# First pair of graphs: four PSUM buffers, both graphs side by side, adjacency loaded into idle buffers, weights loaded later

## The chip, the cores and the metric

The kernel runs on one core of a Trainium2 chip. The metric is the device time of one execution in microseconds (us). Before the change it is 3160.63 us, the median of three runs (3157.54 to 3173.24). PE is the matrix engine (PEld its weight loads), DVE the vector engine, ACT the scalar engine, POOL the general one; SP only issues DMAs here. L with a number is a line of the kernel before; lines of the changed kernel are named as such.

## What is computed

Sixteen graphs of 1024 nodes with 64 features each pass two layers; each adds its result to its input. Cut to what matters:

```python
# layer 0: thin out the neighbours, then take quantiles over those that stay
neigh = (adj > 0) & ~eye;  rank = cumsum(neigh) - neigh;  nb = neigh.sum(-1)
skip = where(nb > 10, (nb + 1) // 2, 1)
rem = neigh & (skip > 1) & (rank % skip == skip - 1) & mask;  rem = rem | rem.T
nd = where(rem, 0, adj with ones on its diagonal) > 0
s = sort(where(nd, h, inf))                   # h = relu(layernorm(x)); per node and feature
agg = 0.25 * quantile(s, 0.25) + 0.5 * quantile(s, 0.5) + 0.25 * quantile(s, 0.75)
x = x + (relu((h + agg) @ W1 + b1) @ W2 + b2) * mask
# layer 1: three graph convolutions  relu(adj @ (x @ W) + b), each with batch norm, then Wl
```

## The kernel before, in words

**Pairs and stages.** The graphs are handled in eight pairs. For each pair there is a preparation (`prepare`, L585) and then seven blocks of nodes, ordered by degree, each gathered and sorted. `prepare` loads x, does the layernorm (`room`, L560 to L568), stores h, and calls `prepare_one` (L654) for each graph of the pair, one after the other. That has these steps, and yields between them:

1. Eight row blocks of the adjacency (`a`, 128x1024 f32, 512 KB, two buffers; L664, issued by SP). ACT takes the sign into `edge` (L671), DVE checks that all values are 0 or 1 (`junk_v` and `odd`, L673), PE turns the block over in eight 128x128 products (`ptE`, L678), ACT evicts it into `edgeT` (L681).
2. `edgeT` is stored to memory for layer 1 (`adjT_d`, L684); then DVE clears its diagonal (L686), which overwrites what the store reads and so waits for it. `chunk_sums` (PE `tot` L646, ACT `sums` L651), then the degrees (`nbp` L691, and small DVE operations L695 to L707 that give `back` and `look`).
3. For each of eight row blocks: PE forms running counts (`cs`, L716 and L721), ACT evicts them as `stays` (L725), DVE compares (L726).
4. For each row block: PE adds up the parts (`q`, L736 to L747), ACT evicts the live edges into `edge` with a count (`nv`, L752).
5. The nodes are ranked by their number of neighbours: `key` (L758), PE spreads it (`keys`, L763), eight ACT passes count who lies above (L770), and `place` (L773) is the rank.
6. POOL scatters the rows of `edge` to memory by `place` (`live_d`, L778), eight DMAs.
7. `find_live` (L788): POOL fetches the rows back in their new order (`lp`, two buffers, L794), PE turns them over (`pt` L809), ACT evicts them into `liveT` (L812), then sums, `nvs` (L822) and a check of bounds (`by` L829, evicted at L833).
8. `number_slots` (L838): PE numbers the live neighbours of each node (`pr`, L845 and L847), ACT evicts them into `r0` (the first 592 nodes) or `r1` (L851). `r0` is done in `prepare`, `r1` in `st.number`, which is worked off during the first sort of the pair.

`prepare` ends with the quantile positions `z` (L615 to L618) and `hp`, h split into three bf16 parts (L623 to L628). Then a gather makes one-hot matrices on DVE (`s`, L987) and multiplies them on PE (`pg`, L1018); sort networks on DVE (L935) follow.

**What sets the order.** Each engine works through its instructions in one fixed order, which a scheduler at compile time makes from the order in which the code is written and from its own estimate of the durations. For the first pair the written order is `prepare`, then the first gather, with nothing beside them. From then on `weave` (L1106) steps the preparation of the next pair and the gather of the next block between the sort's instructions, by shares. After the last pair's gather begins, `later` does the dense layers in the same way; it is the only reader of the weights.

**PSUM.** In `prepare` all of `ptE`, `tot`, `nbp`, `cs`, `q`, `keys`, `pt`, `pr` and the like share one tag, `big`, with two buffers of two banks each, in the pool `ps_early`. The rest of PSUM belongs to the pool `ps` of the gather.

**Weights.** Before anything else is written, ACT's queue issues 46 small DMAs with all weights and biases (`weight`, `column`, `row`, `both`, L496 to L518), and DVE and ACT fold the batch norm into a scale and a shift (`bn_s`, L531 to L537). ACT's first passes over the graphs stand behind these in its order.

**Buffers.** The pools `work` (tags `s`, `agg` and others) and `rows` (tags `g`, `t`) belong to gather and sort, and hold nothing while the first pair is prepared.

Of the kernel before, what the change touches and what calls it, by code (L numbers as in the profile page):

```python
# [10 lines left out]
F32 = mybir.dt.float32  # L11
F16 = mybir.dt.float16
BF16 = mybir.dt.bfloat16
F8 = mybir.dt.float8e4
I32 = mybir.dt.int32
U8 = mybir.dt.uint8
AF = mybir.ActivationFunctionType
ALU = mybir.AluOpType
# [4 lines left out]
P = 128  # L23
# [6 lines left out]

SHARES = (10, 9, 17, 24, 20, 13, 0)
STEPS = 7

MAGIC = 8388608.0

# [344 lines left out]
class Steps:  # L380


    def __init__(self, gen):
        self.gen, self.result = gen, None
# [13 lines left out]
            pass  # L398


@with_exitstack
def graph_layers_kernel(ctx: ExitStack, tc: tile.TileContext, ins, out: bass.AP):
    nc = tc.nc
# [89 lines left out]

    odd = const.tile([P, NB, NT], F32, name="odd")

    def weight(name, rows, cols, twice=False):  # L496
        t = const.tile([rows * (1 + twice), cols], F32, name=f"w_{name}")
        for k in range(1 + twice):
            nc.scalar.dma_start(out=t[k * rows : (k + 1) * rows, :], in_=ins[name])
        return t  # L500

    def column(name, rows, twice=False):
        t = const.tile([rows * (1 + twice), 1], F32, name=f"c_{name}")
        for k in range(1 + twice):
            nc.scalar.dma_start(out=t[k * rows : (k + 1) * rows, :], in_=ins[name].rearrange("(p o) -> p o", o=1))
        return t

    def row(name, cols):
        t = const.tile([P, cols], F32, name=f"r_{name}")
        nc.scalar.dma_start(out=t, in_=ins[name].partition_broadcast(P))  # L510
        return t

    def both(t, src):

        nc.vector.memset(t, 0.0)
        for k in range(2):
            half = slice(k * C, (k + 1) * C)
            nc.scalar.dma_start(out=t[half, half], in_=src)  # L518


    w1 = weight("L0_gnn_W1", C, HID, True)
    w2 = weight("L0_gnn_W2", HID, C)
    b1 = column("L0_gnn_b1", HID)
    b2 = row("L0_gnn_b2", C)
    layers = []
    for i in (1, 2, 3):
        wl = const.tile([P, P], F32, name=f"wl{i}")
        both(wl, ins[f"L1_gnn_W{i}"])
        bl, g, be, m, v = (column(f"L1_gnn_{k}{i}", C, True) for k in ("b", "g", "be", "m", "v"))
        s = const.tile([P, 1], F32, name=f"bn_s{i}")  # L530
        nc.vector.tensor_scalar(s, v, BN_EPS, None, ALU.add)  # L531
        nc.scalar.activation(s, s, AF.Sqrt)
        nc.vector.reciprocal(s, s)
        nc.vector.tensor_tensor(s, s, g, ALU.mult)

        nc.vector.tensor_tensor(m, m, s, ALU.mult)
        nc.vector.tensor_tensor(be, be, m, ALU.subtract)  # L537
        layers.append((wl, bl, s, be))
    wlast = const.tile([P, 3, P], F32, name="wlast")
    for i in range(3):  # L540
        both(wlast[:, i, :], ins["L1_gnn_Wl"][i * C : (i + 1) * C, :])
    blast = row("L1_gnn_bl", C)

    biases = {}

# [8 lines left out]
    def rows_of(ap):  # L554
        return ap.rearrange("(t p) c -> p t c", p=P)
# [26 lines left out]
        pass  # L582


    def prepare(p, pools):  # L585


        work, keep, ps = pools
        st = Pair()
        st.p = p  # L590
        room = work.tile([P, 4, 2, NT, C], F32, tag="stays", name="room")
        xt, h, sq = room[:, 0], room[:, 1], room[:, 2].rearrange("p x t c -> p (x t) c")
        for x in range(2):
            nc.sync.dma_start(out=xt[:, x], in_=rows_of(x_d[2 * p + x]))
        flat = "p x t c -> p (x t) c"
        layernorm_relu(work, h.rearrange(flat), xt.rearrange(flat), sq, T2)
        for x in range(2):
            nc.sync.dma_start(out=rows_of(h_d[2 * p + x][:, :]), in_=h[:, x])
        yield
        st.g = {}  # L600
        st.nvs = keep.tile([P, N], BF16, tag="nvs", bufs=2, name="nvs")
        r0 = keep.tile([P, 2, NT, SPLIT], BF16, tag="r0", name="r0")
        r1 = keep.tile([P, 2, NT, N - SPLIT], BF16, tag="r1", name="r1")
        st.r = (r0, r1)
        find_live, number_slots = [], []
        for x in range(2):
            find_live.append((yield from prepare_one(st, x, pools)))
        for x in range(2):
            number_slots.append((yield from find_live[x]()))
            yield from number_slots[x](0)  # L610


        st.z = keep.tile([P, len(TAUS), N], BF16, tag="z", name="z")
        half = work.tile([P, N], F32, tag="a", bufs=2, name="half")
        nc.vector.tensor_scalar(half, st.nvs, 0.498, MAGIC, ALU.mult, ALU.add)  # L615
        nc.vector.tensor_scalar(half, half, MAGIC, None, ALU.subtract)
        for q, (tau, _) in enumerate(TAUS):
            nc.vector.scalar_tensor_tensor(st.z[:, q, :], st.nvs, -tau, half, ALU.mult, ALU.add)  # L618
        yield

        h = work.tile([P, 2, NT, C], F32, tag="a", bufs=2, name="h_again")
        for x in range(2):
            nc.sync.dma_start(out=h[:, x], in_=rows_of(h_d[2 * p + x][:, :]))  # L623
        st.hp = keep.tile([P, 3, 2, NT, C], BF16, tag="hp", bufs=2, name="hp")
        nc.scalar.copy(st.hp[:, 0], h)
        nc.vector.tensor_tensor(h, h, st.hp[:, 0], ALU.subtract)
        nc.scalar.copy(st.hp[:, 1], h)
        nc.vector.tensor_tensor(st.hp[:, 2], h, st.hp[:, 1], ALU.subtract)  # L628
        yield
        st.number = itertools.chain(*(number_slots[x](1) for x in range(2)))  # L630
        return st

    def diagonal(e):

# [19 lines left out]
    def prepare_one(st, x, pools):  # L654
# [5 lines left out]
        edge = work.tile([P, NT, N], F8, tag="byte", bufs=4, name="edge")  # L660
        edgeT = work.tile([P, NT, N], F8, tag="byte", bufs=4, name="edgeT")
        def load(t):
            a = work.tile([P, N], F32, tag="a", bufs=2, name="a")
            nc.sync.dma_start(out=a, in_=adj_d[b, t * P : (t + 1) * P, :])  # L664
            return a
# [3 lines left out]
        for t in range(NT):  # L669
            a, coming = coming, load(t + 1) if t + 1 < NT else None  # L670
            nc.scalar.activation(edge[:, t, :], a, AF.Sign, saturate=False)  # L671
            junk = work.tile([P, N], F8, tag="junk_v", name="junk_v")
            nc.vector.scalar_tensor_tensor(  # L673
                junk, a, 1.0, a, ALU.is_equal, ALU.not_equal, accum_out=odd[:, b, t : t + 1], saturate=False
            )
            pt = ps.tile([P, NT, P], F32, tag="big", bufs=2, name="ptE")
            for u in range(NT):
                nc.tensor.matmul(  # L678
                    out=pt[:, u, :], lhsT=edge[:, t, u * P : (u + 1) * P], rhs=ident_h, start=True, stop=True
                )  # L680
            nc.scalar.activation(edgeT[:, :, t * P : (t + 1) * P], pt, AF.Copy, saturate=False)  # L681
            yield

        nc.sync.dma_start(out=adjT_d[b][:, :, :], in_=edgeT)  # L684
        own = diagonal(edgeT)
        nc.vector.tensor_tensor(own, own, other_h[:, None, :].to_broadcast([P, NT, P]), ALU.mult, saturate=False)  # L686
        yield
# [43 lines left out]
        for t in range(NT):  # L731
            q = ps.tile([P, N], F32, tag="big", bufs=2, name="q")
            for hf in range(NH):
# [15 lines left out]
                        start=False, stop=(u % 4 == 3),  # L749
                    )  # L750

            nc.scalar.activation(  # L752
                edge[:, t, :], q, AF.Relu, bias=bias(-2.0), accum_out=nv[:, t : t + 1], saturate=False
            )
            yield

        key = work.tile([P, NT], F32, tag="key", name="key")
# [30 lines left out]
        def find_live():  # L788
# [16 lines left out]
            for t in range(NT):  # L805
                lp, coming = coming, fetch(t + 1) if t + 1 < NT else None
                pt = ps.tile([P, NT, P], F32, tag="big", bufs=2, name="pt")
                for u in range(NT):
                    nc.tensor.matmul(  # L809
                        out=pt[:, u, :], lhsT=lp[:, u * P : (u + 1) * P], rhs=ident_h, start=True, stop=True  # L810
                    )
                nc.scalar.activation(liveT[:, :, t * P : (t + 1) * P], pt, AF.Copy, saturate=False)  # L812
                yield

            half = slice(x * C, (x + 1) * C)
# [22 lines left out]
            def number_slots(side):  # L838

                j0, j1 = ((0, SPLIT), (SPLIT, N))[side]  # L840
                for u in range(NT):
                    pr = ps.tile([P, N], F32, tag="big", bufs=2, name="pr")
                    for a in range(j0, j1, HALF):
                        sl, o = slice(a, min(a + HALF, j1)), slice(a - j0, min(a + HALF, j1) - j0)
                        nc.tensor.matmul(out=pr[:, o], lhsT=upto, rhs=liveT[:, u, sl], start=True, stop=(u == 0))  # L845
                        if u:
# [1 line left out]
                                out=pr[:, o], lhsT=before[:, u : u + 1].to_broadcast([P, P]), rhs=sums[:, sl],  # L848
                                start=False, stop=True,
                            )  # L850
                    nc.scalar.copy(st.r[side][:, x, u, :], pr[:, : j1 - j0])  # L851
                    if u % 2:
                        yield

# [420 lines left out]
    def general(stack):  # L1275
# [37 lines left out]
        with tc.For_i(0, NB) as b:  # L1313
# [102 lines left out]
            ahead.rest()  # L1416
            Steps(next_layer((one, ps), [out[b]], [adjT], xt, ahead.result)).rest()


    with ExitStack() as stack:  # L1420
        keep = stack.enter_context(tc.tile_pool(name="keep", bufs=1))
        pools = (
            stack.enter_context(tc.tile_pool(name="work", bufs=1)),
            stack.enter_context(tc.tile_pool(name="ps", bufs=1, space=PSUM)),
            stack.enter_context(tc.tile_pool(name="rows", bufs=1)),
        )
        last = len(BLOCKS)
        with ExitStack() as inner:
            early = (
                inner.enter_context(tc.tile_pool(name="early", bufs=1)), keep,  # L1430
                inner.enter_context(tc.tile_pool(name="ps_early", bufs=1, space=PSUM)),
            )
            ahead = Steps(prepare(0, early))
            ahead.rest()
            st = ahead.result
            first, *_ = gather_block(st, 0, pools)
            first.rest()
            for p in range(NP - 1):
# [7 lines left out]
                for n in range(last):  # L1446
# [16 lines left out]
                    else:  # L1463
                        weave(sort_block(st, n, pools), gather_block(st, n + 1, pools), steps)
                st = to_come
            for _ in st.number:
                pass

# [69 lines left out]
```

## Time and profile before

The profiled execution took 3163.56 us; its span, from the first to the last instruction, is 3161.8 us.

| what | value |
|---|---|
| median of the runs | 3160.63 us |
| profiled execution / span | 3163.56 / 3161.8 us |
| PE busy | 2599.2 us (82%), 27849 matmuls |
| DVE busy | 2559.8 us (81%) |
| ACT busy | 1696.2 us (54%) |
| POOL busy | 619.5 us (20%) |
| moved | 177.45 MB |
| mean granted PE clock | 0.915 |

The table of slices of a profile divides the span into 40 equal parts and gives the busy share of each engine in tenths. A row of the timeline reads: start, duration, engine, line, operation, out<-in with their sizes, count, and in brackets the idle time before it and what ended that (`<-DMA a<-in_adj`: a load of the tile `a`). Several like instructions in a row are merged, with their whole stretch as the duration. A row of the windows gives a stretch, its length, and for each engine its busy time in it with the number of instructions.

### The profile page before, as it was taken

How to read it: one execution, taken by the hardware profiler on the slowest of the kernel's cores; microseconds unless marked ns; L12 is line 12 of the kernel's file. 1: busy time of each engine (PE TensorE's matmuls, PEld its weight loads, DVE VectorE, ACT ScalarE, POOL GpSimd, SP SyncE). 2: the span in 40 equal slices, each digit the busy share in tenths (PEclk: the TensorE clock that was granted, in tenths of full speed). 3: DMA queues.
4: the chain of work that ended last, by engine and by line, in shares of the span. 5: the costliest groups of instructions: out<-in, count | busy, mean ns of one | idle time of the engine just before them, and what ended most of it. 6: DMA issues, size and time to landing. Idle time of an engine off the chain costs nothing.

```text
span 3161.8 us, 67201 instructions
## 1 busy us (share of the span) xinstructions
PE 2599.2 (82%) x27849; PEld 1697.4 (54%) x27849; DVE 2559.8 (81%) x5895; ACT 1696.2 (54%) x3292; POOL 619.5 (20%) x545
## 2 busy tenths in 40 slices
PE   2678978898888889885798889888986688977778
PEld 1445655565556556653565566456643456644445
DVE  4149889998999799989998999899976979963332
ACT  4764666567557755774367557745853223332221
POOL 5110161022102200330022103300422530311110
PEclk9779999999899999997899999999987799988989
DMA  4131022111211212122111211211113011122211
GB/s 138 46 104 60 3 67 70 56 55 52 66 57 54 64 56 68 46 72 47 42 64 51 66 56 57 67 56 63 48 36 75 9 41 26 49 55 54 54 54 42
DMA packets 221082, 177.45 MB, mean 56 GB/s; under 512 B 189024, under 2 KB 189152, under 8 KB 216672
## 3 DMA queue, kind: packets, MB, share of 16 engines
q1 hardware_dynamic: 141824, 125.88, 13.1%
q0 software_dynamic: 17408, 37.81, 3.9%
q10 hardware_dynamic: 61536, 9.39, 1.7%
q8 instruction: 219, 3.59, 0.5%
q14 instruction: 95, 0.78, 0.1%
HBM read 124.44 MB, written 48.55 MB: 55 GB/s over the span
## 4 chain that ended last, share of the span: by engine, by line
DVE 40%; PE 29%; ACT 12%; DMA 8%; issue 6%; another core or an unknown queue 2%; POOL 2%; ACTq 1%; DVEq 0%; POOLq 0%; SPq 0%
PE pg L1018 11%; DVE t L935 10%; DVE s L987 9%; DVE g L935 8%; PE pg L1200 5%; ACT junk L770 3%; DMA a<-in_adj 3%; DMA lp<-live_d 3%; DVE junk_v L673 2%; PE pr L845 2%; DVE g_tails L935 1%; DVE t_tails L935 1%; PE keys L763 1%; PE pf L1216 1%
## 5 line engine op out<-in xcount | busy, mean ns | idle before, releaser
L1018 PE MATMUL pg<-s,hp 128*64 128x400 bf16 (+11 forms) x16848 | 1366.5, 313 | 172.3 <-DVE s L987 138.1
L1018 PEld LDWEIGHTS <-hp 128*64 128x64 bf16 x16848 | 894.5, 112 | 553.9 <-issue 109.6
L987 DVE TENSOR_SCALAR s<-r 128x3200 bf16<-128x3200 bf16 (+25 forms) x1312 | 623.6, 521 | 103.6 <-PE pg L1018 74.9
L778 POOL DMA_INDIRECT live_d<-edge,place x128 | 261.1, 2040 | 1354.3 <-DVE place L773 1149.9
L1023 ACT COPY g<-pg 128x400 f32<-128x400 f32 (+10 forms) x384 | 169.0, 443 | 399.4 <-PE pg L1018 363.1
L935 DVE TENSOR_TENSOR t<-g 128x600 f32<-128x600 f32 (+9 forms) x524 | 315.5, 626 | 34.0 <-ACT g L1023 33.2
L1200 PE MATMUL pg<-adjT,xw 128*64 128x512 fp8e4 x2304 | 284.5, 398 | 52.8 <-ACT xw L1185 25.7
L935 DVE TENSOR_TENSOR g<-t 128x96 f32<-128x96 f32 (+16 forms) x555 | 283.2, 537 | 1.2
L1243 POOL DMA_INDIRECT agg<-agg_d,place x128 | 171.2, 1338 | 495.2 <-PE pt L1131 258.2
L671 ACT ACTIVATE edge<-a 128x1024 fp8e4<-128x1024 f32 x128 | 135.1, 1058 | 214.4 <-DMA a<-in_adj 213.9
L1200 PEld LDWEIGHTS <-xw 128*64 128x64 bf16 x2304 | 140.1, 114 | 182.4 <-issue 42.0
L868 ACT ACTIVATE coef<-z,bias 128x200 f32<-128x200 bf16 (+6 forms) x480 | 173.9, 405 | 102.3 <-DVE agg L950 66.0
L935 DVE TENSOR_TENSOR t<-t 128x192 f32<-128x192 f32 (+20 forms) x447 | 207.8, 475 | 0.2
L871 ACT ACTIVATE coef<-coef,wcol 128x200 f32<-128x200 f32 (+7 forms) x512 | 189.6, 403 | 9.3 <-issue 7.1
L673 DVE SCALAR_TENSOR_TENSOR junk_v<-a 128x1024 fp8e4<-128x1024 f32 x128 | 155.4, 1214 | 24.4 <-DMA a<-in_adj 24.4
L845 PE MATMUL pr<-liveT,upto 128*128 128x512 fp8e4 (+2 forms) x384 | 127.4, 350 | 53.1 <-ACT r L851 46.9
L770 ACT ACTIVATE junk<-keys,minus 128x1024 fp8e4<-128x1024 f32 x128 | 144.3, 1128 | 38.1 <-PE keys L763 34.3
L851 ACT CAST r<-pr 128x592 bf16<-128x592 f32 (+1 forms) x256 | 142.5, 585 | 41.1 <-PE pr L847 32.1
L794 POOL DMA_DIRECT2D lp<-live_d x128 | 89.4, 699 | 376.9 <-PE pt L809 319.3
L812 ACT ACTIVATE liveT<-pt 128x1024 fp8e4<-128x1024 f32 x128 | 130.3, 1034 | 50.5 <-PE pt L809 47.1
L752 ACT ACTIVATE edge<-q,bias 128x1024 fp8e4<-128x1024 f32 x128 | 141.8, 1108 | 22.6 <-PE q L747 22.6
L725 ACT ACTIVATE stays<-cs,back 128x1024 f16<-128x1024 f32 x128 | 136.7, 1111 | 31.1 <-PE cs L721 15.9
(182 smaller groups left out, 3879.4 us busy)
## 6 DMA issues: line engine op xcount, KB each, us to landing
a<-in_adj SPq DMA_DIRECT2D x128, 512.0 KB
adjT_d<-edgeT SPq DMA_DIRECT2D x16, 1024.0 KB
lp<-live_d POOLq DMA_DIRECT2D x128, 128.0 KB
adjT<-adjT_d SPq DMA_DIRECT2D x16, 1024.0 KB
room<-in_x SPq DMA_DIRECT2D x16, 256.0 KB
h_d<-room SPq DMA_DIRECT2D x16, 256.0 KB
h_again<-h_d SPq DMA_DIRECT2D x16, 256.0 KB
xt<-in_x SPq DMA_DIRECT2D x16, 256.0 KB
```

Source lines behind the costliest of these rows:

```text
L673: nc.vector.scalar_tensor_tensor(junk, a, 1.0, a, ALU.is_equal, ALU.not_equal, accum_out=odd[:, b, t : t + 1], saturate=False)
L770: nc.scalar.activation(junk, keys, AF.Sign, bias=minus[:, t : t + 1], accum_out=above[:, t : t + 1], saturate=False)
L778: sent = nc.gpsimd.indirect_dma_start(out=live_d[b][:, :], out_offset=bass.IndirectOffsetOnAxis(ap=place[:, b, t : t + 1], axis=0), in_=ed ...
L845: nc.tensor.matmul(out=pr[:, o], lhsT=upto, rhs=liveT[:, u, sl], start=True, stop=(u == 0))
L868: nc.scalar.activation(coef[:, i, :], z[:, at], AF.Abs, bias=bias(rank - (slots + 1) // 2 + tau), scale=sign)
L871: nc.scalar.activation(coef[:, i, :], coef[:, i, :], AF.Relu, bias=wcol[:, q : q + 1], scale=-w)
L935: nc.vector.tensor_tensor(view(bufs, o, n1, n2), view(bufs, a, n1, n2), view(bufs, b, n1, n2), ALU.max if op else ALU.min)
L987: nc.vector.tensor_scalar(s[:, k, :, us, w0:], r[:, :, us, at + w0 : at + W], float(LIVE + 1 + k0 + k), None, ALU.is_equal)
L1018: summed = nc.tensor.matmul(out=pg[x * C : (x + 1) * C, ks, w0:], lhsT=st.hp[:, part, x, u, :], rhs=s[:, ks, x, u, w0:], start=(whole and ...
L1023: nc.scalar.copy(g[:, k0 : k0 + n, :], pg)
L1200: nc.tensor.matmul(out=pg[cs, :], lhsT=part[:, u, cs], rhs=adjT[x][:, u, sl], start=(u == 0 and k == 0), stop=(u == NT - 1 and k == len(xw ...
L1243: nc.gpsimd.indirect_dma_start(out=agg[:, t, x, :], out_offset=None, in_=agg_d[b][:, :], in_offset=bass.IndirectOffsetOnAxis(ap=place[:, b ...
```

## The change

It touches the first pair's preparation, the loading of weights, and which pool exists when:

- **PSUM**: the first pair's preparation gets a pool of its own, `ps_first`, in which the tag `big` has four buffers (all eight banks). It is closed before the pools `ps` and `ps_early` are opened. `r1` of the first pair uses `ps_early` with two buffers.
- **Loads**: for the first pair the sixteen row blocks of the adjacency go into sixteen `homes`, buffers of the gather, the sort and `a` that are idle then, all issued right behind x and h instead of two at a time. The compiled SP order is: x (2), eight loads, the two stores of h, eight loads.
- **Side by side**: the steps of the two graphs alternate, graph 1 beginning when graph 0 has turned over its eight row blocks and stored them.
- **Evictions**: for the first pair every second eviction of `edgeT`, of `q`, of `liveT`, of `r0` and of `r1` is on DVE. The store of `edgeT` is issued by ACT, as 32-bit words.
- **Checks**: the sixteen checks of the first pair are written last; in the compiled DVE order they still stand in the first stage, all ahead of graph 0's `look`.
- **Weights**: they are issued by SP behind the first gather of pair 2 (`behind`), in the loop after pair 1's sorts. In the compiled SP order they stand between the fifth and the sixth load of pair 3's row blocks. The batch norm's operations are in the sort of pair 2. The weights' memsets stay early.

```diff
+WEIGHTS = 1
+def side_by_side(one, other):
+    while one.step():
+        other.step()
...
+    behind = None
+    def load_weight(t, src):
+        tc.add_manual_dep(
+            nc.sync.dma_start(out=t, in_=src).ins, behind.ins.name,
...
     def weight(name, rows, cols, twice=False):
...
-            nc.scalar.dma_start(out=t[k * rows : (k + 1) * rows, :], in_=ins[name])
+            load_weight(t[k * rows : (k + 1) * rows, :], ins[name])
...
-    def prepare(p, pools):
+    def prepare(p, pools, homes=()):
...
+        for k, home in enumerate(homes):
+            nc.sync.dma_start(out=home, in_=adj_d[2 * p + k // NT, k % NT * P : (k % NT + 1) * P, :])
...
+        if homes:
+            one, other = (Steps(prepare_one(st, x, pools)) for x in range(2))
+            for _ in range(4 + NT):
+                one.step()
+            side_by_side(one, other)
+            find_live = Steps(one.result())
+            side_by_side(find_live, other)
+            other.rest()
+            number_slots.append(find_live.result)
+            find_live = Steps(other.result())
+            side_by_side(Steps(number_slots[0](0)), find_live)
+            find_live.rest()
+            number_slots.append(find_live.result)
+            yield from number_slots[1](0)
+            for k, home in enumerate(homes):
+                check(2 * p + k // NT, k % NT, home)
...
+    def evict(st, t, o, i):
+        if st.homes and t % 2:
+            nc.vector.tensor_scalar(o, i, 1.0, None, ALU.mult, saturate=o.dtype != F8)
+        else:
+            nc.scalar.activation(o, i, AF.Copy, saturate=o.dtype != F8)
...
-            nc.scalar.activation(edgeT[:, :, t * P : (t + 1) * P], pt, AF.Copy, saturate=False)
+            evict(st, t, edgeT[:, :, t * P : (t + 1) * P], pt)
...
-        nc.sync.dma_start(out=adjT_d[b][:, :, :], in_=edgeT)
+        if st.homes:
+            nc.scalar.dma_start(out=adjT_d[b][:, :, :].bitcast(I32), in_=edgeT.bitcast(I32))
+        else:
+            nc.sync.dma_start(out=adjT_d[b][:, :, :], in_=edgeT)
...
+            if st.homes and t % 2:
+                nc.vector.tensor_scalar(
+                    edge[:, t, :], q, 3.0, 0.0, ALU.is_equal, ALU.add, accum_out=nv[:, t : t + 1], saturate=False
+                )
...
-                nc.scalar.activation(liveT[:, :, t * P : (t + 1) * P], pt, AF.Copy, saturate=False)
+                evict(st, t, liveT[:, :, t * P : (t + 1) * P], pt)
...
-                    nc.scalar.copy(st.r[side][:, x, u, :], pr[:, : j1 - j0])
+                    evict(st, u, st.r[side][:, x, u, :], pr[:, : j1 - j0])
...
+            homes = []
+            for pool, tag, bufs, free in (
+                (rows, "g", 2, 2), (rows, "g", 2, 2), (rows, "t", 1, 3), (work, "s", 2, 3), (work, "s", 2, 3),
+                (work, "agg", 1, 1), (room, "a", 2, 1), (room, "a", 2, 1),
+            ):
+                home = pool.tile([P, free, N], F32, tag=tag, bufs=bufs, name="home")
+                homes += [home[:, k] for k in range(free)]
+            with tc.tile_pool(name="ps_first", bufs=1, space=PSUM) as ps_first:
+                ahead = Steps(prepare(0, (room, keep, Deep(ps_first, 4)), homes))
+                ahead.rest()
             st = ahead.result
+            pools = work, stack.enter_context(tc.tile_pool(name="ps", bufs=1, space=PSUM)), rows
+            early = room, keep, inner.enter_context(tc.tile_pool(name="ps_early", bufs=1, space=PSUM))
+            st.ps = early[2]
...
                 st = to_come
+                if p != WEIGHTS:
+                    continue
+                behind = st.gathered
...
+                w1 = weight("L0_gnn_W1", C, HID, True)
...
```

## The prediction

> **What bounds the kernel now.** I read the table of 40 slices first (79 us each). DVE is at 9 in most slices; in the first three it is at 4, 1 and 4: there something else sets the pace.
>
> ```profile
> PE   2678978898888889885798889888986688977778
> DVE  4149889998999799989998999899976979963332
> ACT  4764666567557755774367557745853223332221
> PEclk9779999999899999997899999999987799988989
> ```
>
> So only the time until the first gather (some 206 us) is at stake, and from there a lead gained is passed on, because PE and DVE are busy for 189 and 192 us of the 220 between 280 and 500 and follow each other. The windows by stage show what fills the prologue:
>
> ```profile
> 32.00:67.00 35.00, 12.23 (x99) 8.29 (x100) 17.88 (x31) 22.60 (x24) 11.52 (x60) 1.00 0.69 223
> 67.00:91.00 24.00, 19.70 (x186) 13.25 (x184) 7.65 (x18) 20.75 (x28) 0.00 (x0) 1.00 0.15 50
> 91.00:109.00 18.00, 9.12 (x80) 7.88 (x81) 0.18 (x2) 15.77 (x23) 0.00 (x0) 0.67 0.00 1
> 109.00:143.00 34.00, 23.84 (x221) 15.52 (x220) 6.40 (x17) 20.21 (x27) 8.94 (x10) 0.77 0.20 70
> 143.00:161.00 18.00, 8.90 (x80) 7.86 (x80) 2.96 (x5) 15.59 (x23) 3.22 (x6) 0.65 0.28 74
> 161.00:191.00 30.00, 19.08 (x123) 9.82 (x124) 2.87 (x4) 17.97 (x25) 12.75 (x16) 0.61 0.37 106
> ```
>
> Columns: stretch, length, busy us of PE, weight load, DVE, ACT, POOL, then granted clock, DMA share, GB/s. No engine is full; the stages run one after another. The timeline gives the marks that I count from:
>
> ```profile
> 31.57 1.06 ACT L563 ACTIVATE room<-room 128x1024 f32<-128x1024 f32 x1 [1.74 <-DMA wlast<-in_L_gnn_Wl]
> ```
> ```profile
> 67.08 1.10 ACT L725 ACTIVATE stays<-cs,back 128x1024 f16<-128x1024 f32 x1
> ...
> 93.22 1.11 ACT L770 ACTIVATE junk<-keys,minus 128x1024 fp8e4<-128x1024 f32 x1 [2.40 <-PE keys L763]
> ```
> ```profile
> 161.33 0.17 DVE L773 TENSOR_SCALAR place<-above 128x8 int32<-128x8 f32 x1 [12.62 <-ACT junk L770]
> ...
> 195.56 0.69 DVE L615 TENSOR_SCALAR half<-nvs 128x1024 f32<-128x1024 bf16 x1 [29.14 <-ACT nvs L822]
> ...
> 205.80 1.89 DVE L987 TENSOR_SCALAR s<-r 128x3200 bf16<-128x3200 bf16 x2
> ```
>
> ACT does no work on the graphs until 31.57: it issues weights, 46 DMAs at 0.607 us each, 28 us. First `stays` at 67.08, first ranking pass at 93.22, `place` of the two graphs at 109.09 and 161.33, first one-hot `s` at 205.80.
>
> **Edge stage.** The weights leave ACT's head, so ACT starts with the first row block, which landed 4.4 us after its issue. Now DVE is the limit, because the compiled order has all sixteen `odd` checks ahead of graph 0's `look`: 16 x 1.15 (their pitch in the trace) = 18.4; layernorm 1.22+0.2+1.22+1.22+0.25+1.23 = 5.3; constants 2.1; four evictions; the diagonal product 1.25; memsets and small operations 2.5. A DVE eviction from PSUM is not in the trace: its 1024-element f32 rows lie between 0.69 (`half`) and 1.22 (`junk_v`). I take 1.2, since ACT's 1.02 for the same tile lies nearer to it; 4.8 (at 0.69: 2.8). Sum 34.3, from 4.8. The product must wait for the store of `adjT` (4.5 alone; up to 8 beside the loads): some 2 us more. So first `stays` at 41 instead of 67.1: **lead 26**. Loads: 8.4 MB ran at 223 GB/s with two in flight (38 us), single short slices of the trace reach 396 (21 us); the check of the last block comes at 40, so only the slow end costs, up to 5. A second table load (1.28) lies on ACT, which has room.
>
> [...]
>
> **Side by side.** Each later stage is a chain in one engine's order, and the order now mixes two graphs.
> - `stays` and q: 8 x 1.06 + 1.0 on ACT, then what the trace has from last `stays` to `key` (78.7 to 90.84, 12.2) plus six `ptE` groups of graph 1 on PE at 0.6: 3.6. Graph 0's `key` at 41 + 9.5 + 15.8 = 66.3, lead 24.5. Half the q evictions on DVE bring nothing: PE needs 1.4 per block, ACT 1.2 to 1.3.
> - `keys`. PE's order has graph 1's `tot` and `nbp` ahead of graph 0's `keys`. Graph 1's `edgeT` is stored only about 1.5 before `key`; then store 4.6, product 1.25, `tot` 1.9, `sums` 1.05, `nbp` 0.4, `keys` 2.06: first ranking pass at 76.1. **Lead 17**: 7 us go to a new wait. The passes alternate with graph 1's `stays` as they did with its `edgeT`: 15.9, `place` at 92.
> - First `pt`. Scatter and fetch take 12.4 + 2.4 = 14.8 in the trace: 106.8. PE has this `pt` ahead of graph 1's last two `cs`, so it stands still for about 10 us where the old order ran graph 1 under graph 0's scatter. Then `pt` 1.0, two `cs` of 1.7 each (their pace at 119 to 123, with the clock of 0.67 in the stage before), `stays`, `not_equal`, a DVE eviction: 6.8; eight q at 1.4, six `pt` at 0.6, `tot` 1.5, last eviction 1.3: 17.6. Graph 1's `key` at 131.2 against 143.10: **lead 12**.
> - Ranking of graph 1: no longer alternating with eight `liveT` (18.2), but with two `r`, a square and a root: 2.4 + 8.8 + 1.1 + 1.4, and some 1.5 until the first `pr`: 15.2. `place` at 146.4, lead 15.
> - Scatter, fetch, `liveT` of graph 1: fetch-bound (two `lp` buffers, `pt` waits up to 3.3 us on DMA), so split evictions and more PSUM bring nothing: 29.4 as before, 0.5 for graph 0's `pr` between. To the first `s`: 15.05 as before, plus 1, as DVE now has four `r` evictions and all of `z` ahead of `s`. **First `s` at 192, lead 13.5.** Bounds: 4 (slow loads and stores) and 26 (no later loss).
>
> **What is given back behind it.** Eight of the first pair's sixteen `r1` evictions (128x432) go from ACT to DVE, seven of them beside its sort, where DVE is busy 47.4 of 50 us: 7 x 0.5 (0.49 is 432/1024 of 1.15) = 3.5, bounds 0 and 7, as PE holds two `pr` buffers and may wait behind DVE's order. The weights' fifteen small DVE operations now stand in the sort of pair 2: 15 x 0.16 = 2.4, bounds 2 and 5 (three roots on ACT between them). The weights themselves go to SP's queue, which they hold for 28 us between the fifth and the sixth row block of pair 3, with its `mk` and `adjT` store behind them. In the trace the gather that they wait for ends at 838 and the fifth block is issued near 841; the first `v` would land at 841 + 17 x 0.607 + 2 = 853, and DVE comes to its use at 853.6, to the second (861 against 860.6) and the third (868 against 868) about in time. The next check stands some 30 DVE rows later than before. I take 0, bounds 0 and 28.
>
> Sum: 13.5 - 3.5 - 2.4 = 7.6 us. From the profiled execution (3163.6; span 3161.8 and 1.8 around it) 3156; the median of the runs is 2.9 lower: **3153**.
>
> **Rivals.**
> 1. The lead of 26 survives: the two waits in PE's order prove shorter than priced, because the store and the scatter land sooner. For it: PE, DVE and ACT all have room in the prologue; against it: 14.8 and 4.5 us are measured with DMA nearly idle. 26 - 6 = 20: 3141.
> 2. Slower: SP's queue. If its 46 weight issues come later than DVE's rows for them (from a lag of about 1 us, as the three marks show), DVE stands for the rest, at worst all 28 us: 13.5 - 6 - 28 = -20.5: 3181. For it: all three marks are within 1 us, and `a` loads and DVE are in the same fixed order. Against it: each further `v` is due 7 us after the last, as fast as they are issued.
> 3. The change does nothing that lasts: the first gather starts early, but pair 1's preparation does not (in the first 1000 us SP waits 194.8 us until `edgeT` can be stored), and the lead is lost at the first change of pairs: 3160 to 3166.
>
> **Chances.** Forecast 0.50, rival 1 0.27, rival 2 0.11, rival 3 0.12. The measurement tells some 0.5% (15.8 us) from no change: faster is rival 1 and 0.05 of the forecast's own spread, 0.32; slower is rival 2, 0.11; the rest, 0.57. The range takes in rival 1 and rival 3 and the bounds of the lead, and leaves out rival 2: 3134 to 3172; the forecast's own is 3145 to 3160.
>
> **What would show it.** First `edge` on ACT near 6 us instead of 32; first `stays` at 41; `keys` waiting for `nbp`, first ranking pass at 76; PE idle about 10 us ahead of the first `pt` near 107; first `s` at 192; seven `r1` evictions on DVE within the first sort; no DVE wait on `c_L_gnn_v` over 2 us. A first `s` ahead of 185 makes rival 1, a wait of DVE or ACT on weights or on `a` of over 15 us rival 2.

## The result and the profile after

The changed kernel takes 3166.87 us (median of 20 runs, 3144.34 to 3182.04), the kernel before on the same chip 3167.34 us (20 runs, 3156.96 to 3176.8): ratio **0.9996**, 95% interval 0.9978 to 1.0014. No difference can be told. A second set on another chip gave 0.9974 (0.9950 to 0.9997). The median of before differs between the chips used here (3167, 3134, 3139 and 3134 us), so below only ratios to it, times on one chip and times inside one profile are compared.

The profiled execution took 3148.95 us, its span is 3147.2 us. It is the second shortest of the 20; of its 14.6 us less than before's span a part is luck. The 40 slices of its page, 79 us each:

```profile
PE   5379888888898788984987889888986689977778
DVE  6279889998999799999997999799986979963332
PEclk9789899999999899987998999899986899988889
```

DVE's first three digits are 6, 2, 7 instead of 4, 1, 4: the prologue did shrink. The windows of its stages (busy us of PE, weight load, DVE, ACT, POOL, then clock, DMA share, GB/s):

```profile
7.00:42.40 35.40, 15.83 (x128) 10.62 (x129) 29.77 (x65) 22.90 (x25) 22.90 (x57) 1.00 0.71 256
...
75.40:91.00 15.60, 5.59 (x61) 3.82 (x58) 3.10 (x7) 15.01 (x22) 0.02 (x1) 0.81 0.00 1
91.00:106.40 15.40, 1.04 (x9) 0.99 (x10) 0.00 (x0) 0.00 (x0) 8.92 (x10) 0.50 0.25 85
...
141.00:157.00 16.00, 1.39 (x10) 1.12 (x11) 0.17 (x1) 1.42 (x3) 8.95 (x11) 0.50 0.52 148
```

The edge stage is now full of DVE (29.8 of 35.4 us). But there are two stretches of some 15 us, 91 to 106 and 141 to 157, in which little but POOL's scatters and fetches runs; the other engines stand nearly idle. The marks, from ACT's and then DVE's timeline:

```profile
6.88 1.06 ACT L706 ACTIVATE edge<-home 128x1024 fp8e4<-128x1024 f32 x1 [4.84 <-DMA home<-in_adj]
...
42.39 6.13 ACT L762 ACTIVATE stays<-cs,back 128x1024 f16<-128x1024 f32 x6 [4.04 <-DVE bias L544]
...
75.44 1.11 ACT L812 ACTIVATE junk<-keys,minus 128x1024 fp8e4<-128x1024 f32 x1 [3.74 <-PE keys L805]
...
106.44 1.02 ACT L664 ACTIVATE liveT<-pt 128x1024 fp8e4<-128x1024 f32 x1 [15.95 <-PE pt L851]
```
```profile
141.01 0.17 DVE L815 TENSOR_SCALAR place<-above 128x8 int32<-128x8 f32 x1 [0.82 <-ACT junk L812]
...
182.81 1.89 DVE L1029 TENSOR_SCALAR s<-r 128x3200 bf16<-128x3200 bf16 x2
```

The first `s` stands at 182.81 instead of 205.80: **23 us earlier** (187.44 in a second profile of it: 18). So the question is where some 20 us went. To follow them I number ACT's copies `g<-pg`, whose order is the same in every kernel here, and compare the time between two of them. About half of all stretches of four copies agree within 1 us in the four profiles, and a single profile can be off by up to 10 us. Behind the first eight copies, both changed profiles differ from both of before by more than 4 us in two places only, those of the last two rows:

| stretch (copies) | before, two profiles | changed, two profiles |
|---|---|---|
| start to first copy | 213.6, 213.1 | 192.4, 196.4 |
| start to 48 (pair 1's sort) | 520.7, 523.0 | 500.5, 500.8 |
| 103 to 107 | 17.7, 18.5 | 25.0, 26.1 |
| 132 to 140 | 82.4, 71.9 | 86.4, 89.8 |

With the pairs counted from 0, some 20 to 22 us are passed on into pair 1 and most of it is lost beside the sort of pair 2, where pair 3 is prepared and the weights now load. SP's timeline there, in the changed kernel (first and last of the weights; the code and the traces have 48 of these loads, where the description of before and the prediction say 46; the 28 us for them change by about 1):

```profile
784.73 27.34 SPq L699 DMA_DIRECT2D a<-in_adj  x5
812.12 1.83 SPq L509 DMA_DIRECT2D w_L_gnn_W<-in_L_gnn_W  x3
...
843.91 0.59 SPq L509 DMA_DIRECT2D r_L_gnn_bl<-in_L_gnn_bl  x1
844.93 1.19 SPq L699 DMA_DIRECT2D a<-in_adj  x2
```

And ACT's waits in the same stretch (bracket: idle before, and what ended it):

```profile
815.56 1.06 ACT L706 ACTIVATE edge<-a 128x1024 fp8e4<-128x1024 f32 x1 [0.83 <-DMA a<-in_adj]
...
825.93 0.20 ACT L1538 ACTIVATE bn_s<-bn_s 128x1 f32<-128x1 f32 x1 [0.20 <-DVE bn_s L1537]
...
834.33 0.20 ACT L1538 ACTIVATE bn_s<-bn_s 128x1 f32<-128x1 f32 x1 [5.54 <-DVE bn_s L1537]
...
842.01 0.20 ACT L1538 ACTIVATE bn_s<-bn_s 128x1 f32<-128x1 f32 x1 [6.69 <-DVE bn_s L1537]
...
848.80 1.06 ACT L706 ACTIVATE edge<-a 128x1024 fp8e4<-128x1024 f32 x1 [5.87 <-DMA a<-in_adj]
```

Theories: **C**, the clock gives the lead back (mean granted clock 0.911 over the changed kernel's 20 runs, 0.915 in before's first profile); **W**, the weights' new place costs it; **R**, the `r1` evictions on DVE and the new order beside the first sort cost it.

### The profile page after: what moved, and what is told of

Read it like the earlier page. It is cut to its first block, busy times and chain, and to the rows that moved or that the text cites. A ratio compares the mean times of both kernels' runs of the same rounds, so it can differ in the third digit from the quotient of the medians.

```text
span 3147.2 us, 67155 instructions
## 1 busy us (share of the span) xinstructions
PE 2590.4 (82%) x27826; PEld 1705.3 (54%) x27849; DVE 2596.7 (83%) x5943; ACT 1663.0 (53%) x3245; POOL 614.6 (20%) x545
## 4 chain that ended last, share of the span: by engine, by line
DVE 44%; PE 25%; issue 9%; ACT 9%; DMA 6%; POOL 4%; another core or an unknown queue 2%; SPq 1%; DVEq 0%; POOLq 0%; ACTq 0%
DVE t L977 11%; DVE s L1029 10%; DVE g L977 9%; PE pg L1060 9%; PE pg L1242 5%; DVE junk_v L593 3%; DMA lp<-live_d 3%; ACT junk L812 2%; POOL live_d L820 1%; DVE g_tails L977 1%; DMA a<-in_adj 1%; DVE t_tails L977 1%; PE pt L851 1%; POOL agg L1285 1%
## 5 line engine op out<-in xcount | busy, mean ns | idle before, releaser
L820 POOL DMA_INDIRECT live_d<-edge,place x128 | 246.0, 1922 | 1341.1 <-DVE place L815 1130.8
L1285 POOL DMA_INDIRECT agg<-agg_d,place x128 | 178.3, 1393 | 488.9 <-PE pt L1173 310.7
L706 ACT ACTIVATE edge<-a 128x1024 fp8e4<-128x1024 f32 x112 | 118.3, 1058 | 193.5 <-DMA a<-in_adj 193.3
L664 ACT ACTIVATE liveT<-pt 128x1024 fp8e4<-128x1024 f32 x120 | 122.4, 1034 | 84.3 <-PE pt L851 82.5
L851 PE MATMUL pt<-ident_h,lp 128*128 128x128 bf16 x1024 | 81.8, 228 | 93.1 <-DMA lp<-live_d 83.9
L664 ACT ACTIVATE r<-pr 128x592 bf16<-128x592 f32 (+1 forms) x240 | 136.1, 593 | 38.4 <-PE pr L889 29.3
L1247 DVE TENSOR_SCALAR xT<-xT,bn_s,c_L_gnn_be 128x512 f32<-128x512 f32 x48 | 26.1, 544 | 155.0 <-ACT xT L1246 154.9
```

The lines of the kernel that those rows point to most:

```text
L664: nc.scalar.activation(o, i, AF.Copy, saturate=o.dtype != F8)
L820: sent = nc.gpsimd.indirect_dma_start(out=live_d[b][:, :], out_offset=bass.IndirectOffsetOnAxis(ap=place[:, b, t : t + 1], axis=0), in_=ed ...
L1285: nc.gpsimd.indirect_dma_start(out=agg[:, t, x, :], out_offset=None, in_=agg_d[b][:, :], in_offset=bass.IndirectOffsetOnAxis(ap=place[:, b ...
```

## The experiments

**First group: C against W against R.** `before_again` is the kernel before without an edit. `after_pause` lets the first loads wait for ten small DMAs in a chain:

```diff
+            for _ in range(HOPS):                    # 5
+                nc.sync.dma_start(out=afar[:, :], in_=to_and_fro)
+                nc.sync.dma_start(out=to_and_fro, in_=afar[:, :])
+            nc.vector.tensor_copy(xt[:, 0, 0, :4], to_and_fro)
+            for home in homes:
+                nc.vector.tensor_copy(home[:, :4], to_and_fro)
```

> The kernel before, unchanged, so that each of its runs has a granted clock beside it. Theory C (the clock gives the lead back: after the shorter prologue TensorE is granted less): mean clock 0.914 to 0.918, against 0.911 in the 20 runs of the changed kernel, at the same time of 3167. Theory W (the weights' new place costs what the prologue gains) and theory R (the evictions on DVE and the new order cost it): the clock of both kernels is the same within 0.001, or what differs in it follows from waits.

> The changed kernel with ten small DMAs, each waiting for the last, ahead of the first loads: the prologue starts some 18 to 24 us later, the exact number is read from the first gather's mark; the order behind it is the same on TensorE. If the end follows the prologue (theories W and R), it is 3167 + 18 to 24 = 3185 to 3191. Theory C: the delay is mostly given back by the clock, 3167 to 3175.

`before_again`: 0.9999 (0.9978 to 1.0020), mean clock 0.922. `after_pause`: 1.0034 (1.0019 to 1.0049), mean clock 0.921. Its first copy is at 214.9, 20 us later than in the kernel of this chip with the same weights' place (`after_r1_act`, 194.8), and its median is 18.3 us above that kernel's. Idle time put into the prologue arrives at the end almost whole, at the same clock. C falls. (Within one chip the clock of the changed kernel is a little lower, 0.919 against 0.922 in the set with 0.9974; in `after_w_early` below it is 0.922 as before, so this goes with the waits and not with the early start.) The run also prices what is given back: its first `s` stands at 206.12, where before has 205.27, so that it has no lead, and it is 0.0034 (10.7 us, 6 to 15) slower than before.

`after_w_early` issues the weights on SP in the prologue, behind the row blocks and graph 0's mask (first fence, shortened); `after_r1_act` takes the `r1` evictions back to ACT (second fence):

```diff
             for _ in range(4 + NT):
                 one.step()
+            load_weights()      # the 48 loads, without the wait for st.gathered
```
```diff
-                    evict(st, u, st.r[side][:, x, u, :], pr[:, : j1 - j0])
+                    evict(st, u * (1 - side), st.r[side][:, x, u, :], pr[:, : j1 - j0])
```

> The changed kernel with its 46 weight loads on SP in the prologue, behind the row blocks of the first pair, instead of in the middle of the later pair's row blocks; their few operations stay in the later pair. Theory W (SP's queue, held for 32 us between two row blocks of pair 3, costs the lead): 10 to 20 us faster than the changed kernel, 3147 to 3157. Theories C and R: as the changed kernel, 3163 to 3170.

> The changed kernel with all r1 evictions of the first pair on ACT again. My price for them on DVE was 3.5 us (0 to 7). Theory R (these evictions and the new order of pair 0 cost the lead): 5 to 15 us faster, 3152 to 3162. Theories C and W: 0 to 3.5 faster, 3163 to 3167.

`after_w_early`: **0.9935** (0.9914 to 0.9956), 21.6 us under before. `after_r1_act`: 0.9982 (0.9966 to 0.9998), not to be told from the changed kernel's two ratios. On one chip the two differ by 15.3 us, and only in the weights' place and the `r1` evictions. W holds; R has nothing to show.

**Second group: what in the weights' place costs.** Two candidates beside SP's held queue itself (W3). W1: the three roots (`bn_s`) stand in ACT's order among pair 3's evictions and wait for weights. W2: the scheduler, which had to place the new operations, made another order for pair 3. POOL's timeline of the changed kernel:

```profile
1022.80 0.54 POOL L836 DMA_DIRECT2D lp<-live_d  x1 [1.47 <-PE pt L851]
1023.64 1.37 POOL L820 DMA_INDIRECT live_d<-edge,place  x1 [0.30 <-DVE g L977]
...
1034.17 2.04 POOL L820 DMA_INDIRECT live_d<-edge,place  x1 [0.30 <-issue]
1036.21 1.15 POOL L836 DMA_DIRECT2D lp<-live_d  x2
```

The last two fetches of the first graph stand behind the eight scatters of the second. PE has their `pt` next, and stands; its own row (first) and the windows show that, and the clock around it:

```profile
1038.62 1.89 PE L851 MATMUL pt<-ident_h,lp 128*128 128x128 bf16 x16 [8.62 <-DMA lp<-live_d]
```
```profile
1028.00:1030.00 2.00, 0.37 (x2) 0.14 (x1) 2.00 (x9) 0.51 (x3) 1.39 (x3) 1.00 0.18 66
1030.00:1032.00 2.00, 0.00 (x0) 0.00 (x0) 2.00 (x15) 0.52 (x2) 1.70 (x2) 0.66 0.55 169
...
1036.00:1038.00 2.00, 0.00 (x0) 0.00 (x0) 1.99 (x3) 0.00 (x0) 1.36 (x3) 0.50 0.41 123
...
1042.00:1044.00 2.00, 2.00 (x17) 0.39 (x20) 0.00 (x0) 0.59 (x3) 0.00 (x0) 0.50 0.20 66
1044.00:1046.00 2.00, 2.00 (x23) 0.98 (x24) 0.00 (x0) 1.25 (x3) 0.00 (x0) 0.93 0.04 8
```

In before and in `after_w_early` all eight fetches come ahead of these scatters. `after_again` is the changed kernel without an edit. `after_ops_late` moves only the batch norm's folding (DVE and ACT) one pair later; the loads stay. `after_fetch_first` pins only the order of pair 3, with a dependency that orders the schedule and makes no engine wait (shortened):

```diff
+        st.sent.append(rows_sent)
...
+                if st.p == WEIGHTS + 2 and x == 0 and t == NT - 1:   # last fetch of graph 0
+                    for sent in st.sent[1]:                          # scatters of graph 1
+                        tc.add_manual_dep(
+                            sent.ins, load.ins.name,
+                            mybir.DependencyInfo(mybir.DependencyClass.NoSync, mybir.DependencyReason.SCHED_ONLY),
+                            reason="the other graph's rows behind these",
+                        )
```

> The changed kernel, unchanged, on the chip of the next three, as their reference and as a second profile of it. Expected from the first runs: 0.995 to 1.000 of the kernel before; in its profile the three roots of the weights on ACT wait some 12 us among the evictions of pair 3, and TensorE stands 8 to 10 us for a fetch of live_d near 1030, with the granted clock at 0.50 behind it, as in three profiles with the weights in that place.

> The changed kernel with the weights' loads where they are, in SP's queue between the row blocks of pair 3, but their operations on DVE and ACT one pair later, so that no root waits on ACT; the compiled order then has all eight fetches of pair 3's first graph ahead of the second graph's scatters again. Theory W1 + W2 (the roots' wait, 6 to 7 us, and the two fetches behind eight scatters, 8 to 10 us): 13 to 16 us faster than the changed kernel. Theory W3 (SP's held queue is the cost): no faster than the changed kernel, within 4 us.

> The changed kernel with one thing in its order pinned: in pair 3 the second graph's scatters on POOL stand behind the last fetch of the first graph. W2 alone goes: 8 to 10 us faster than the changed kernel, the wait of TensorE near 1030 under 3 us; the roots' wait stays. If the order of these fetches does not matter (W1 or W3 alone): within 4 us of the changed kernel.

| kernel | ratio (95%) | copies 103 to 107 | 132 to 140 |
|---|---|---|---|
| `after_again` | 0.9974 (0.9950 to 0.9997) | 26.1 | 89.8 |
| `after_ops_late` | 0.9950 (0.9930 to 0.9969) | 25.8 | 76.9 |
| `after_fetch_first` | 0.9957 (0.9939 to 0.9975) | 26.3 | 82.5 |
| `after_w_early` | 0.9935 (0.9914 to 0.9956) | 19.0 | 77.1 |

W1 was wrong: without the roots the first stretch is as long, because ACT then waits at the next place for the same queue. In `after_ops_late`:

```profile
852.91 1.06 ACT L706 ACTIVATE edge<-a 128x1024 fp8e4<-128x1024 f32 x1 [12.15 <-DMA a<-in_adj]
```

So **SP's held queue costs 7 us** there (25.8 against 19.0), with or without the roots. All fourteen profiles bear this out: 25.0 to 26.3 in the six with the weights in that place, 17.7 to 19.6 in the eight others.

**The order of the fetches costs some 8 us** in the second stretch. From 132 to 140 the three profiles of this set give 7 to 13 (89.8 against 82.5 and 76.9), with the first profile of the changed kernel (86.4) 4 to 10. The part where PE stands, copies 136 to 140, is sharper: the four profiles with two fetches behind the scatters have 37.4 to 38.2, the ten others 25.3 to 33.1, on the mean 37.7 against 29.3. PE's wait of 8.6 us (9.3 and 9.5 in the two others with this order) is gone in `after_fetch_first`:

```profile
1031.64 0.62 PE L859 MATMUL pt<-ident_h,lp 128*128 128x128 bf16 x8 [1.90 <-DMA lp<-live_d]
```

A wait of 5.20 us comes there at 1052.73, for the second graph's first rows. The medians point the same way (5.7 and 4.1 us below the changed kernel, where 13 to 16 and 8 to 10 were expected), but their intervals overlap; the marks carry this reading, not the medians. 7 and 8 add up to the 15.3 us between `after_w_early` and `after_r1_act`.

`before_w_sp` is the kernel before with one part of the change: the weights leave ACT's head. They go to SP, behind the first pair's second `adjT` store; the batch norm's operations stand in the sort of pair 2, as in the change (shortened).

```diff
-            nc.scalar.dma_start(out=t[k * rows : (k + 1) * rows, :], in_=ins[name])
+            load_weight(t[k * rows : (k + 1) * rows, :], ins[name])   # SP, behind stored[1]
```

> The kernel before with one part of the change alone: the 46 weight loads leave ACT's head. They go to SP's queue behind the first pair's loads and store; their operations stand in the later pair. One graph after the other, two buffers, all evictions on ACT as before. If ACT's head is what the prologue waits for: first stays near 45 instead of 67, first gather 15 to 25 us earlier, and 12 to 22 us faster than before, about what the whole change brings with the weights early. If the graphs side by side and the idle buffers are what brings it: under 8 us.

0.9934 (0.9909 to 0.9958), 19.1 us. Its first `stays` and first `s`:

```profile
43.03 1.11 ACT L729 ACTIVATE stays<-cs,back 128x1024 f16<-128x1024 f32 x1
```
```profile
182.22 1.89 DVE L991 TENSOR_SCALAR s<-r 128x3200 bf16<-128x3200 bf16 x2
```

This one part makes the whole of the earlier first gather; the buffers, PSUM, evictions and the mixed graphs add nothing to it in sum.

**Third group: why the rest adds nothing, and the better version.** In the changed kernel PE waits for the fetches of both graphs in turn, first 22.4 and then 22.1 us. The lines of before and of the changed kernel (us in total, times, longest; from 60 to 190):

```profile
PE pt L809 <- DMA lp<-live_d: 8.7, 4, 3.3
```
```profile
PE pt L851 <- DMA lp<-live_d: 48.5, 6, 22.4
```

`w_early_in_turn` is `after_w_early` with the first pair's graphs one after the other, and the weights behind all of graph 0's preparation; `w_early_pin` and `before_w_sp_pin` pin the fetches in every later pair, because before's own order has the last fetches of the first graph behind the scatters in pairs 1 and 5; `in_turn_pin` has both.

```diff
-            side_by_side(one, other)
...
+            for x in range(2):
+                one = Steps(prepare_one(st, x, pools))
+                one.rest()
+                find_live.append(one.result)
+                if not x:
+                    load_weights()
+            for x in range(2):
+                number_slots.append((yield from find_live[x]()))
+                yield from number_slots[x](0)
```

> The changed kernel with the weights early on SP and the first pair's graphs one after the other, as in the kernel before; the idle buffers, the four PSUM buffers and the evictions on DVE stay. My prediction had two losses in the order side by side: the first ranking pass 7 us late behind graph 1's sums, 5 more at the first pt. If they are real, the first gather starts 4 to 8 us earlier than with the graphs side by side and the weights early (187.97 there), near 181, and the time is 0.991 to 0.993 of before. If side by side pays what it was made for, the first gather starts later than 192 and the time is 0.995 or more.

> The kernel before with the weights on SP behind the first pair's loads (0.9934 alone), and the order on POOL pinned in all later pairs: the second graph's scatters behind the last fetch of the first. In the order of before, pairs 1 and 5 have the last two fetches behind the eight scatters. If each costs what it cost in pair 3 (5 to 10 us): 0.989 to 0.991. If the stall is covered there: 0.993 to 0.994.

> The changed kernel with the weights early on SP (0.9935) and the same pin in all later pairs. If the fetches cost in pairs 1 and 5 as well: 0.989 to 0.991; if covered: 0.993 to 0.994. It also tells the other parts of the change from the weights alone: level with the kernel before with weights on SP and the pin if they bring nothing, 5 us or more ahead of it if they bring something that the weights' place hid.

> Weights early on SP, graphs in turn, idle buffers, four PSUM buffers, evictions on DVE, and the pin: the best that the runs so far point to. 0.987 to 0.991, if what each brings adds up: 4 to 8 us from the order in turn, 0 to 15 from the pin, on top of 0.9935.

| kernel | ratio (95%) | first `s` | copies 41 to 48 | 228 to 240 |
|---|---|---|---|---|
| `after_w_early` | 0.9935 (0.9914 to 0.9956) | 187.97 | 67.7 | 115.9 |
| `w_early_pin` | 0.9871 (0.9843 to 0.9898) | 189.65 | 58.6 | 109.9 |
| `w_early_in_turn` | 0.9870 (0.9842 to 0.9897) | 167.64 | 70.8 | 115.1 |
| `before_w_sp_pin` | 0.9884 (0.9856 to 0.9912) | 180.66 | 60.3 | 107.1 |
| `in_turn_pin` | **0.9816** (0.9780 to 0.9852) | 165.66 | 58.8 | 108.7 |

The order in turn brings 20 us at the first `s`, against the 4 to 8 expected. The same line of `w_early_in_turn`:

```profile
PE pt L860 <- DMA lp<-live_d: 22.8, 7, 11.1
```

Graph 0's scatter and first fetches lie under graph 1's `cs` and `q` again; side by side, nothing was left to run under them, the first empty stretch above. The marks place the gain: with the graphs in turn the first ranking pass stands at 63.24 instead of 74.69 (`after_w_early`), `place` of the two graphs at 76.84 and 121.78 instead of 90.37 and 141.62. From there to the first `s` both take some 46 us, so the second empty stretch is no cost of the order side by side. The pin brings 6 to 12 us in each of the two pairs that had the bad order (on the mean of all profiles with and without it 10 and 8). All four ratios lie below the low end of what was expected (that of `before_w_sp_pin` by less than its interval): the signs were right and the sizes too small. `in_turn_pin` is 57 us under before. With the pin and in turn, the other parts (idle buffers, four PSUM buffers, evictions on DVE) do bring something: first `s` 15 us ahead of `before_w_sp_pin`, median 3076.75 against 3099.48 us. I did not part them from each other.

## Why the prediction was wrong, step by step

- **Edge stage.** First `stays` at 41 forecast, 42.39 measured. Right, and DVE is the limit, as said; a DVE eviction of 128x1024 from PSUM takes 1.22 us, 1.2 were taken. Within the sum two terms are off and cancel: DVE waits 4.77 us for the store of `adjT`, where some 2 were taken, and is busy for 31.8 us, where 34.3 were summed. That the two `a` buffers of before reach 43.03 without the rest was not seen: the rest of the stage's parts was not needed for this lead.
- **`keys` and first `pt`.** First ranking pass 76.1 forecast, 75.44 measured; first `pt` at 106.8 forecast, its eviction at 106.44. The waits are the ones named, but larger: PE stands 22.4 us ahead of this `pt`, where I had about 10, because it was through with what it could do of graph 1 at 83. As the `pt` itself comes on time, that did not move the mark.
- **From there to the first `s`.** 192 forecast, 182.81 and 187.44 measured: graph 1's `key` came at 126.56 instead of 131.2, and the end took less. Lead 18 to 23 instead of 13.5, inside the bounds of 4 to 26: this term was 5 to 10 us too small. A first `s` ahead of 185 was my mark for rival 1; it appeared in one profile, and the time of rival 1 did not, because the mark only looks at the prologue.
- **"From there a lead gained is passed on".** Right until pair 3 is prepared: 20 to 22 us at copy 48. Rival 3 named the time (3160 to 3166) with the wrong place: the lead is not lost at the first change of pairs.
- **`r1` evictions on DVE, 3.5, and the small operations, 2.4.** Neither shows, though the 432 wide evictions take 0.6 us each and not 0.5: `after_r1_act` can't be told from the changed kernel.
- **"I take 0, bounds 0 and 28"**, for SP's queue: this is the step that failed. It costs 7 us. I had compared DVE's `v` with its landing, and there it was right: DVE waits 1.3 to 2.2 us for each `v` in the two profiles. I had left out who else stands in line: ACT's roots, and behind them the sixth row block, which ACT takes up 33 us after the fifth (848.80 against 815.56) and in before 26 (870.67 against 844.21).
- **What the sum left out.** I counted the moved operations by their durations and not by what they do to the compiled order. The fetches behind the scatters cost some 8 us more, in a place where no line of the diff stands. Of 18 to 23 us of lead, 7 and some 8 are given back: 3 to 8 remain, which the two ratios (1.3 us by 0.9996, 8.2 by 0.9974) can't tell from nothing. That the upper end comes to the 7.6 us of the prediction is luck: a lead sized too small stands against two costs put at nothing.
- **The choice of rivals.** I priced the mixed order against before's order with the weights in front. The right comparison is the old order with the weights gone from ACT's head: against it the whole rest of the change brings nothing to the first `s` (`before_w_sp`, 182.22), and with nearly all else alike side by side loses 20 us (`w_early_in_turn`).
- **The weights' issues.** The prediction counted 28 us of ACT for them. Taken off ACT's head, the 48 small loads bring 19 us (`before_w_sp`); put on SP between two row blocks, they hold it for 32 us (812.12 to 844.50).

## What to carry to other kernels

A moved block had two prices here, its own issues in the new queue (7 us) and the order that the scheduler then made around it (some 8 us): compare the orders queue by queue (here POOL's scatters and fetches), not only the diff. Before mixing two chains, list which waits each now covers for the other; with the two graphs in step, nothing of graph 1 was left to cover graph 0's scatter (PE was busy for 1.04 of 15.4 us). When several parts change at once, ask what the simplest one alone gives: here it gave the whole earlier first gather, and the order side by side hid what other parts bring.

## What the runs showed of the hardware

In the first profile of the changed kernel PE works at half its clock for a while behind two long waits. Nearly idle from 1028 on, PE loses the full clock near 1030.6, and after it resumes at 1038.62 the clock is back only near 1044.3, 5.7 us later. Behind the wait of 22.42 us in the prologue (from 82.95) the clock is gone near 85.1, and back near 109.0, 3.7 us after PE resumes at 105.36.

In the first profile of before, ACT, DVE and PE stop one after the other between 751.8 and 753.6 with nothing that the profile shows to wait for, while POOL goes on:

```profile
754.00:756.00 2.00, 0.00 (x0) 0.00 (x0) 0.00 (x0) 0.00 (x0) 1.70 (x2) 0.96 0.37 131
756.00:758.00 2.00, 0.70 (x3) 0.37 (x5) 1.74 (x14) 0.74 (x3) 1.39 (x3) 0.50 0.19 68
...
766.00:768.00 2.00, 2.00 (x11) 0.66 (x8) 0.12 (x1) 0.90 (x3) 0.00 (x0) 0.50 0.00 0
```

ACT's `g<-pg` there has 4.51 us of idle time put down to issue. The same place in `before_again` has no such stop, and the clock stays at 1.00. With the clock at 0.50 from 755.9 to 769.5, copies 88 to 96 take 69.0 us instead of 61.3. A second stop stands in the same profile near 1055 (DVE idle for 7.06 us before 1061.15, put down to `remote`); it lies in the stretch 132 to 140 and is most of why that is 82.4 there and 71.9 in `before_again`. That such stops are one source of the runs' spread is my estimate, from these 7.7 and 10.5 us between the two profiles; what causes them stays open.
